# A two-layer graph attention kernel: own rows added by VectorE in the early sums, and written by ScalarE into opened accumulators in layer 0

## Chip, cores and metric

The kernel runs on one core of one Trainium2 chip. The metric is device time in microseconds of that core. A core has five engines with a queue each, worked off in order: TensorE (PE; PEld is its weight load), VectorE (DVE), ScalarE (ACT), GpSimd (POOL) and SyncE (SP). SP issues plain transfers, POOL the gathers of rows by index. Sixteen DMA engines move the data. TensorE sums into PSUM banks of 512 f32 columns.

## What is computed

N = 3327 nodes with D = 1024 features, a symmetric 0/1 adjacency with ones on its diagonal and about 17 ones in a row. Layer 0 is attention with 8 heads of 128 columns, layer 1 with one head. After each comes a residual add and a layer norm. Cut to what matters:

```python
# layer 0
h = (x @ W).reshape(C, H, D); h_heads = jnp.transpose(h, (1, 0, 2))
e = alpha_src[:, :, None] + alpha_dst[:, None, :]
e = jnp.where(e >= 0, e, NEG_SLOPE * e)            # 0.2
e = jnp.where(adj[None] == 0, -jnp.inf, e)
out = jnp.einsum('hij,hjd->hid', softmax(e, axis=-1), h_heads)
x = _layernorm(x + out)
# layer 1: the same with one head, leaky 0.2, and relu(attention @ h)
x = _layernorm(x + layer1(x))
```

The attention of a node is a weighted sum over its neighbours and over itself. The "own row" below is the node's own row of h, weighted by the node's own, unnormalised attention weight (zero where the diagonal is zero).

## The kernel before

The rows lie in 26 tiles of 128 (NT = 26; NTH = 13). The work has three stages.

**Projection** (L512 to L927). For each tile t, `project` multiplies the turned x by W0 in three column cuts of eight matmuls; `keep` has ScalarE move the result out of PSUM, and SP stores it in the table h0_d, each row followed by exponentials of its scores. `load_mask` brings a tile's adjacency as bytes with POOL's queue into one of three buffers, 416 KB. Three generators run beside the projection, and `pace()` (L629), called after every second matmul, gives them their turn. I call each call of `pace()` a slot: there are twelve per tile. In a slot:

- `counting` (L580) clears a mask's diagonal and sums it on ScalarE (L348), then packs it on VectorE (L355). It gets a turn in every third slot.
- `listing` (L592) finds a tile's neighbours: VectorE searches maxima (L307, L309), ScalarE and TensorE spread them, and the lists go to idx, tgt and re_d. It takes seven steps a tile, 187 in all, and `pace` sets how many are due: 3/7 of them in the first half of the projection, the rest in the second.
- `sums_so_far` (L646), from tile 13 on, forms for the EARLY = 17 first tiles the part of layer 0 that comes from neighbours in the first half of the rows. A tile has two blocks of four gathers from h0_d (L660, buffers near and far); per block `weights` computes e on VectorE (L677, L678, L681) and `sums` adds up 32 small matmuls for each half of the heads (L690). Then ScalarE copies both banks of the sum to z and the denominators to dens (L738, L739), and SP stores z in half_d (L740). A tile takes nine slots.

**Layer 0** (`pipeline`, L1322 on, with the class Layer0, L1059). The tiles come in an order that mixes early tiles (blocks 2, 3 and the end block 4; the other two are in half_d) and nine late ones (all five blocks). A block is four gathers of 128 rows of 4160 bytes (the end block one), into one of five buffers; `send` issues a gather as soon as a buffer is free. For a tile, `prepare` is called in the middle of the tile before: it loads x (y), the tile's own rows of h0_d (own, L1075) and, for an early tile, half_d (half, L1078). At the tile's first block `own` computes the own weights on VectorE (L1084 to L1090), and `scale_own` has ScalarE scale the own rows by head (L1097). `sums` has TensorE multiply the weights of a block with its rows (L1147; the end block at L1138), and in the second and third block adds the scaled own rows and the half sum to the accumulators by an f32 matmul with the identity (L1130). The denominators lie in den. `finish` divides, adds the residual, normalises, computes layer 1's scores, and SP stores the row in y_d (L1190).

**Layer 1** (class Target, L1199 on) gathers rows of y_d in five blocks per tile (L1258), then multiplies the normalised sum by W1 (L1290).

The scheduler's order is that of the program: everything runs in a manual schedule, so each engine's queue is the order in which these generators issue. A wait in one engine's queue holds everything behind it on that engine.

The lines around L1130 in `sums` of layer 0:

```python
if j in (1, 2):
    for rows_ in (self.h, self.half) if self.t < EARLY else (self.h,):
        nc.tensor.matmul(
            self.acc[j - 1].rearrange("p h d -> p (h d)"), ident, rows_[:, (j - 1) * HALF : j * HALF],
            start=False, stop=False,
        )
elif j == 3:
    nc.tensor.matmul(self.acc[0][:, 0, :1], ident_b, none_b, start=False, stop=False)
```

Of the kernel before, what the change touches and what calls it, by code (L numbers as in the profile page):

```python
# [19 lines left out]
P = 128  # L20
# [6 lines left out]
def kernel(  # L27
# [102 lines left out]
    dens = const.tile([P, EARLY, H], F32, name="dens")  # L130
    io_t = const.tile([P, P], F32, name="io_t")

    near = [const.tile([P, NG, HG], F32, name=f"near{b}") for b in range(HB)]

# [377 lines left out]
    with ExitStack() as own, tc.manual_schedule():  # L512
# [14 lines left out]
        def load_mask(t):  # L527
            if t < NT:
                ads[t] = masks[t % 3]
                if t == NT - 1:  # L530
                    nc.vector.memset(ads[t].bitcast(I32), 0)
                    nc.vector.memset(ads[t][:, :1], 1.0)
                for r in pieces(t):
                    nc.gpsimd.dma_start(ads[t][r, :N], adj[at(t, r), :])
# [94 lines left out]
        def pace():  # L629
# [3 lines left out]
            if n % 3 == 0:  # L633
                next(counts, None)
            first = 3 * total // 7
# [10 lines left out]
        def sums_so_far():  # L646
# [52 lines left out]

            res = [listed(0), listed(1)]  # L700
            for _ in range(3):
                yield
            for n in range(2):
                fetch(n)
                yield
                yield
                yield
# [4 lines left out]
            for s in range(EARLY):  # L712
                acc = part.bank("L", [P, 2, 4, DH], "part")
                made = []
                for b in range(HB):
                    n = s * HB + b
                    val = src[n % 3]
                    made.append(weights(val, b, res[0], oh))
                    yield
                    if n:  # L720
                        fetch(n + 2)
# [4 lines left out]
                    if b == 0:  # L726
                        yield
                        yield
# [7 lines left out]
                z = part.sbuf("z", [P, 2, 4, DH], 1)  # L736
                for n in range(2):
                    nc.scalar.activation(z[:, n], acc[:, n], AF.Copy)  # L738
                nc.scalar.activation(dens[:, s, :], den, AF.Copy)  # L739
                nc.sync.dma_start(half_d[s], z.rearrange("p n h d -> p (n h d)"))  # L740
# [5 lines left out]
                yield  # L746

# [19 lines left out]
        masks = [pool.tile([P, NP], U8, bufs=1, name=f"ad{n}") for n in range(3)]  # L767
# [107 lines left out]
        for t in range(3, NT):  # L875
# [3 lines left out]
            if t == 12:  # L879
# [11 lines left out]
            if t == 16:  # L891
                nc.gpsimd.tensor_copy(loop, own_a)
# [79 lines left out]
    def sparse(own):  # L972
# [7 lines left out]
        grows = pool.tile([P, NT, H], F32, bufs=1, name="grows")  # L980
        nc.scalar.activation(grows, sd0[:, :, 0, :], AF.Exp, scale=1 - SLOPE)
# [9 lines left out]
        none_b = pool.tile([P, 1], BF16, name="none_b")  # L991
        nc.vector.memset(none_b, 0.0)
# [66 lines left out]
        class Layer0:  # L1059
# [9 lines left out]
            def prepare(self):  # L1069
# [4 lines left out]
                self.h = sbuf("own", [P, HW0], 2)  # L1074
                nc.sync.dma_start(self.h, h0_d[self.t * P : (self.t + 1) * P, :HW0])  # L1075
                if self.t < EARLY:
                    self.half = sbuf("xT", [P, KT, P], 2, "half").rearrange("p k q -> p (k q)")
                    nc.sync.dma_start(self.half, half_d[self.t])  # L1078

            def own(self):  # L1080

                t, h = self.t, self.h
                es, total = sbuf("es0", [P, 2, H], 2).rearrange("p a h -> a p h")
                nc.vector.tensor_tensor(es, grows[:, t, :], h[:, D : D + H], OP.mult)  # L1084
                nc.vector.tensor_tensor(es, es, h[:, D + H :], OP.max)
                nc.vector.tensor_scalar(es, es, loop[:, t : t + 1], None, op0=OP.mult)
                self.es = self.total = es
                if t < EARLY:
                    self.total = total
                    nc.vector.tensor_tensor(total, es, dens[:, t, :], OP.add)  # L1090

            def scale_own(self):

                h = self.h
                for n in range(H):
                    d = slice(n * DH, (n + 1) * DH)
                    nc.scalar.activation(h[:, d], h[:, d], AF.Copy, scale=self.es[:, n : n + 1])  # L1097

            def begin(self):
                self.acc = [bank("A", [P, 4, DH], "acc") for _ in range(2)]  # L1100
# [22 lines left out]
            def sums(self, b):  # L1123
# [4 lines left out]
                if j in (1, 2):  # L1128
                    for rows_ in (self.h, self.half) if self.t < EARLY else (self.h,):
                        nc.tensor.matmul(  # L1130
                            self.acc[j - 1].rearrange("p h d -> p (h d)"), ident, rows_[:, (j - 1) * HALF : j * HALF],
                            start=False, stop=False,
                        )
                elif j == 3:
# [10 lines left out]
                for h in range(H):  # L1145
                    for g in range(NG):
                        nc.tensor.matmul(  # L1147
                            self.acc[h // 4][g * GT : (g + 1) * GT, h % 4, :], e[:, g, h, :], rowsof[:, g, h, :],
                            start=first and h % 4 == 0, stop=False,
# [16 lines left out]
            def finish(self):  # L1166

                ri = sbuf("ri", [P, H], 2)
                nc.vector.tensor_tensor(ri, self.den, self.total, OP.add)
# [29 lines left out]
        class Target:  # L1199
# [29 lines left out]

            def scale_own(self):  # L1230
                pass
# [90 lines left out]
        def pipeline(items, fetches):  # L1322
# [28 lines left out]
            get(0)  # L1351
            items[0].prepare()
# [5 lines left out]
            items[0].weights(items[0].blocks[0])  # L1358
            for i, it in enumerate(items):
# [4 lines left out]
                for j, b in enumerate(it.blocks):  # L1364
# [8 lines left out]
                    if j == 0:  # L1373
                        get(i + 1)
                    if j == nb // 2 and after:
# [7 lines left out]
                    if j == 0:  # L1383
                        it.scale_own()
# [176 lines left out]
```

## Time and profile before

| | |
|---|---|
| time, median of 3 runs | 1854.35 us (1852.41 to 1872.16) |
| the profiled execution's own time | 1778.88 us |
| its span, first to last instruction | 1777.1 us |
| busy in the span: PE, DVE, ACT, POOL | 1518.3, 1150.6, 537.5, 1111.7 us |
| transferred | 592.41 MB |
| mean granted TensorE clock | 0.926 |

The profile is that of one execution. Busy time is the time that an engine executes; a wait is idle time ahead of an instruction, put down to what ended last. In lists of groups a row gives line, engine, operation, output and input, shape and count, then busy us and mean ns of one, then the idle us ahead of it and what ended it. A matmul in f32 shows as two records. In lists of waits a row gives who waited for whom, us in total, how often, and the longest. In the chain of waits a row gives its start, its us and what it was. A mean over the span hides that the three stages have different limits, so each is looked at by itself.

### The profile page before, as it was taken

To read this page: it belongs to the slowest core of one execution; us is meant where nothing else is said; L and a number is where in the kernel's file an instruction comes from. 1 tells how busy PE (TensorE), PEld (TensorE's weight loads), DVE (VectorE), ACT (ScalarE), POOL (GpSimd) and SP (SyncE) were. 2 spreads that over 40 slices of the span, in tenths; PEclk is the share of its full clock that TensorE was granted. 3 is DMA by queue.
4 is the path that set the end of the run, shared out by engine and by line. 5 is a ranking of instruction groups with operands and counts; after the bars stand their busy time and mean duration, and the time that the engine had idled before them with its cause. 6 is when DMAs were issued, how large, how long until landed. Compare 5 with 4: busy or idle time off the path is not lost.

```text
span 1777.1 us, 36731 instructions
## 1 busy us (share of the span) xinstructions
PE 1518.3 (85%) x13778; PEld 882.2 (50%) x13778; DVE 1150.6 (65%) x3125; ACT 537.5 (30%) x1602; POOL 1111.7 (63%) x1476
## 2 busy tenths in 40 slices
PE   8799999999995667666676674599999999999998
PEld 5466666666664455444554453244444444444443
DVE  6799999888873877767777775243444444444443
ACT  5678773333322233233333332011110111101110
POOL 4443358877755666656656666677676666676750
PEclk9999999999998788888788886899999999999999
DMA  7578978998888999999999999999999999999980
GB/s 195 100 138 167 163 170 302 319 314 319 296 303 331 407 411 408 394 384 406 395 397 393 385 402 365 355 395 403 396 393 386 394 390 396 401 401 395 386 345 36
DMA packets 189050, 592.41 MB, mean 333 GB/s; under 512 B 37069, under 2 KB 47079, under 8 KB 188864
## 3 DMA queue, kind: packets, MB, share of 16 engines
q0 software_dynamic: 131056, 458.88, 72.6%
q1 hardware_dynamic: 57650, 130.84, 19.8%
q8 instruction: 111, 1.82, 0.4%
q14 instruction: 75, 0.61, 0.1%
q10 hardware_dynamic: 158, 0.26, 0.0%
HBM read 590.02 MB, written 53.33 MB: 362 GB/s over the span
## 4 chain that ended last, share of the span: by engine, by line
PE 42%; DMA 18%; DVE 4%; issue 1%; ACT 1%; POOL 1%; DVEq 0%; SPq 0%; POOLq 0%; ACTq 0%
PE mm L1290 21%; PE acc L1258 13%; DMA src<-h_d,idx 7%; DMA own<-h_d 4%; PE acc L1147 3%; DMA near<-h_d,idx 3%; PE acc L1130 3%; DVE e L1115 2%; PE tr L195 1%; DMA src<-y_d,idx 1%; DMA near<-y_d,idx 1%; ACT own L1097 1%; DMA end<-h_d,idx 1%; DVE pr L1002 1%; PE acc L1138 1%
## 5 line engine op out<-in xcount | busy, mean ns | idle before, releaser
L545 PE MATMUL mm<-wt,xT 128*128 128x347 f32 (+1 forms) x1248 | 408.0, 468 | 2.1 <-DMA wt<-in_L_gnn_W_dram 1.5
L1290 PE MATMUL mm<-wt,xT 128*128 128x512 f32 x832 | 387.6, 604 | 0.0
L1036 POOL DMA_INDIRECT src<-y_d,idx x240 | 244.6, 1019 | 95.0 <-issue 32.7
L545 PEld LDWEIGHTS mm<-wt,xT 128*128 128x128 f32 x1248 | 225.7, 192 | 116.7 <-issue 18.4
L1036 POOL DMA_INDIRECT src<-h_d,idx x168 | 180.9, 1077 | 112.4 <-PE acc L1147 25.2
L1290 PEld LDWEIGHTS mm<-wt,xT 128*128 128x128 f32 x832 | 149.7, 189 | 199.1 <-issue 194.1
L1293 DVE SCALAR_TENSOR_TENSOR o<-mm,y 128x512 f32<-128x512 f32 x52 | 36.0, 692 | 317.1 <-PE mm L1290 317.1
L1036 POOL DMA_INDIRECT near<-y_d,idx x176 | 178.9, 1017 | 90.6 <-PE acc L1258 29.7
L1130 PE MATMUL acc<-own,ident 128*128 128x512 f32 x104 | 80.4, 865 | 118.8 <-ACT own L1097 115.2
L1036 POOL DMA_INDIRECT near<-h_d,idx x104 | 116.1, 1117 | 65.1 <-DMA src<-h_d,idx 13.9
L198 ACT ACTIVATE xT<-tr 128x512 f32<-128x512 f32 x104 | 63.2, 609 | 254.1 <-PE tr L195 254.0
L1272 ACT ACTIVATE z<-y,ri 128x342 f32<-128x342 f32 (+1 forms) x78 | 39.5, 569 | 300.5 <-DVE ri L1268 300.5
L660 POOL DMA_INDIRECT near<-h_d,idx x96 | 105.2, 1096 | 36.2 <-issue 24.4
L1120 ACT ACTIVATE w<-way 128x32 f32<-128x32 f32 (+1 forms) x96 | 18.5, 192 | 350.4 <-DVE e L1115 168.6
L1115 DVE TENSOR_TENSOR e<-oh,way 128x1024 f32<-128x1024 f32 x96 | 117.2, 1221 | 8.4 <-DVE way L1113 0.5
L1147 PE MATMUL acc<-src,e 128*32 128x128 f32 x2688 | 103.4, 318 | 17.6 <-DVE e L1115 17.6
L1258 PE MATMUL acc<-src,es 128*32 128x342 f32 (+1 forms) x1440 | 116.2, 454 | 0.2
L1258 PE MATMUL acc<-near,es 128*32 128x342 f32 (+1 forms) x1056 | 90.1, 476 | 28.0 <-DVE es L1249 28.0
L1147 PEld LDWEIGHTS acc<-src,e 128*32 128x32 f32 x2688 | 88.1, 129 | 47.1 <-DVE e L1115 31.9
L1147 PE MATMUL acc<-near,e 128*32 128x128 f32 x1792 | 65.8, 309 | 23.0 <-DVE e L1115 12.2
L348 ACT ACTIVATE junk<-ad 128x1664 uint8<-128x1664 uint8 x52 | 82.9, 1594 | 5.6 <-POOL ad L337 4.0
L1130 PEld LDWEIGHTS acc<-own,ident 128*128 128x128 f32 x104 | 20.4, 245 | 124.6 <-ACT own L1097 123.9
(238 smaller groups left out, 2577.8 us busy)
## 6 DMA issues: line engine op xcount, KB each, us to landing
own<-h_d SPq DMA_DIRECT2D x26, 520.0 KB
y_d<-y SPq DMA_DIRECT2D x26, 514.0 KB
y<-y_d SPq DMA_DIRECT2D x26, 514.0 KB
h_d<-ht SPq DMA_DIRECT2D x25, 520.0 KB
x<-in_x_dram SPq DMA_DIRECT2D x25, 512.0 KB
y<-in_x_dram SPq DMA_DIRECT2D x25, 512.0 KB
out_dram<-o SPq DMA_DIRECT2D x25, 512.0 KB
ad<-in_adj_dram POOLq DMA_DIRECT2D x25, 415.9 KB
```

The lines of the kernel that those rows point to most:

```text
L198: nc.scalar.activation(part, tr, AF.Copy)
L348: nc.scalar.activation(junk, ad[:, n * THR : (n + 1) * THR], AF.Copy, accum_out=self.d[:, n : n + 1])
L545: nc.tensor.matmul(acc, xT[t][:, k, :], wt[:, k, CUTS0[c] : CUTS0[c + 1]], start=k == 0, stop=k == KT - 1)
L660: nc.gpsimd.indirect_dma_start(out=src[n % 3][:, g, :], out_offset=None, in_=h0_d[:THR, :], in_offset=bass.IndirectOffsetOnAxis(ap=idx[:, ...
L1036: nc.gpsimd.indirect_dma_start(out=s[:, g, :w], out_offset=None, in_=table[:n, :], in_offset=bass.IndirectOffsetOnAxis(ap=idx[:, t, b * NG ...
L1115: nc.vector.tensor_tensor(e, oh.unsqueeze(2).to_broadcast([P, ng, H, wide]), wp.unsqueeze(3).to_broadcast([P, ng, H, wide]), OP.mult,)
L1130: nc.tensor.matmul(self.acc[j - 1].rearrange("p h d -> p (h d)"), ident, rows_[:, (j - 1) * HALF : j * HALF], start=False, stop=False,)
L1147: nc.tensor.matmul(self.acc[h // 4][g * GT : (g + 1) * GT, h % 4, :], e[:, g, h, :], rowsof[:, g, h, :], start=first and h % 4 == 0, stop= ...
L1258: nc.tensor.matmul(self.acc[c][to, :m], es[:, g, :], s[:, g, CUTS[c] : CUTS[c + 1]], start=b == 0, stop=b == EB,)
L1272: nc.scalar.activation(z[:, cut], self.res[:, cut], AF.Copy, scale=ri[:, 1:2])
L1290: nc.tensor.matmul(acc, xT[:, k, :], wt1[:, k, half], start=k == 0, stop=k == KT - 1)
L1293: nc.vector.scalar_tensor_tensor(o[:, half], acc, 0.0, res[:, half], op0=OP.max, op1=OP.add)
```

## The change

For the early sums, SP loads each tile's own rows of h0_d into one of two buffers (`own_row`), ScalarE scales them by head with weights computed once for all tiles (`own_terms`, own_e), and VectorE adds the sums in PSUM to them (`settle`), in place of ScalarE's copy. The first half of the head columns is settled behind the tile's last sums, the second one slot later, ahead of the next tile's weights. half_d then holds the early sum with the own row in it, and own_e the denominators.

In layer 0 a tile loads one row block instead of up to two: half_d for an early tile, h0_d for a late one (`load_own`, at the first block of the tile before). In the last block of the tile before, TensorE writes zeros over both accumulators with a bf16 matmul (`open`), and ScalarE writes into them the half sum as it is or the own rows scaled by head (`lay`). The tile's first matmul adds to that. The matmuls with the identity and the own weights computed per tile are gone; the one-column zero matmul comes in the blocks 1 to 3 of a tile's list except the end block.

The pacing is changed with it: counting gets two of five slots in place of one of three, listing has 2/5 of its steps in the first half in place of 3/7, all masks but the last are counted before the early sums begin, the diagonal is loaded at tile 5 (12 before) and converted at tile 11 (16 before), and the three mask buffers are one tile, of which the first part later serves as the second own-row buffer.

```diff
@@ masks, pacing
-                ads[t] = masks[t % 3]
+                ads[t] = masks[(t + 1) % 3]
...
-            if n % 3 == 0:
+            if n * 2 % 5 < 2:
                 next(counts, None)
-            first = 3 * total // 7
+            first = 2 * total // 5
@@ own weights, once for tiles lo to hi
+    def own_terms(lo, hi, mids):
+
+        e, score = own_e[:, lo:hi, :], sd0[:, lo:hi, 1, :]
+        for mid, scale in zip(mids, (1.0, SLOPE)):
+            nc.scalar.activation(mid, score, AF.Exp, scale=scale)
+        nc.scalar.activation(e, sd0[:, lo:hi, 0, :], AF.Exp, scale=1 - SLOPE)
+        nc.vector.tensor_tensor(e, e, mids[0], OP.mult)
+        nc.vector.tensor_tensor(e, e, mids[1], OP.max)
+        nc.vector.tensor_tensor(e, e, loop[:, lo:hi].unsqueeze(2).to_broadcast([P, hi - lo, H]), OP.mult)
@@ early sums
+            def own_row(s):
+                nc.sync.dma_start(own_rows[s % 2], h0_d[s * P : (s + 1) * P, :D])
+
+            def scale(s, n):
+                for h in range(4 * n, 4 * n + 4):
+                    d = slice(h * DH, (h + 1) * DH)
+                    nc.scalar.activation(
+                        own_rows[s % 2][:, d], own_rows[s % 2][:, d], AF.Copy, scale=own_e[:, s, h : h + 1]
+                    )
+
+            def settle(s, n):
+                half = own_rows[s % 2][:, n * HALF : (n + 1) * HALF]
+                nc.vector.tensor_tensor(half, acc[:, n].rearrange("p h d -> p (h d)"), half, OP.add)
+                if n == 1:
+                    nc.vector.tensor_tensor(own_e[:, s, :], own_e[:, s, :], den, OP.add)
+                    nc.sync.dma_start(half_d[s], own_rows[s % 2])
+
+            need(NT - 2)
...
             for s in range(EARLY):
...
+                    if b == 0 and s:
+                        settle(s - 1, 1)
                     made.append(weights(val, b, res[0], oh))
                     yield
+                    if b == 0:
+                        scale(s, 0)
                     if n:
                         fetch(n + 2)
...
                     if b == 0:
+                        scale(s, 1)
                         yield
+                        if s + 1 < EARLY:
+                            own_row(s + 1)
...
-                z = part.sbuf("z", [P, 2, 4, DH], 1)
-                for n in range(2):
-                    nc.scalar.activation(z[:, n], acc[:, n], AF.Copy)
-                nc.scalar.activation(dens[:, s, :], den, AF.Copy)
-                nc.sync.dma_start(half_d[s], z.rearrange("p n h d -> p (n h d)"))
+                if s == EARLY - 1:
+                    yield
+                settle(s, 0)
@@ layer 0
+            def load_own(self):
+                self.h = sbuf("own", [P, D], 2)
+                h0 = h0_d[self.t * P : (self.t + 1) * P, :D]
+                nc.sync.dma_start(self.h, half_d[self.t] if self.t < EARLY else h0)
...
+            def open(self):
+
+                self.acc = [bank("A", [P, 4, DH], "acc") for _ in range(2)]
+                for acc in self.acc:
+                    nc.tensor.matmul(
+                        acc, zero_b, ident_b.unsqueeze(1).to_broadcast([P, 4, P]), start=True, stop=False
+                    )
+
+            def lay(self):
+
+                for n, acc in enumerate(self.acc):
+                    rows_ = self.h[:, n * HALF : (n + 1) * HALF].rearrange("p (h d) -> p h d", h=4)
+                    if self.t < EARLY:
+                        nc.scalar.activation(acc, rows_, AF.Copy)
+                        continue
+                    for h in range(4):
+                        at_h = own_e[:, self.t, 4 * n + h : 4 * n + h + 1]
+                        nc.scalar.activation(acc[:, h, :], rows_[:, h, :], AF.Copy, scale=at_h)
...
-                if j in (1, 2):
-                    for rows_ in (self.h, self.half) if self.t < EARLY else (self.h,):
-                        nc.tensor.matmul(
-                            self.acc[j - 1].rearrange("p h d -> p (h d)"), ident, rows_[:, (j - 1) * HALF : j * HALF],
-                            start=False, stop=False,
-                        )
-                elif j == 3:
+                if 0 < j < 4 and b < EB:
                     nc.tensor.matmul(self.acc[0][:, 0, :1], ident_b, none_b, start=False, stop=False)
...
-                            start=first and h % 4 == 0, stop=False,
+                            start=False, stop=False,
@@ pipeline of layer 0
                     if j == 0:
                         get(i + 1)
+                        if isinstance(after, Layer0):
+                            after.load_own()
...
                     elif after and type(after) is type(it):
                         after.weights(after.blocks[0])
-                    if j == 0:
-                        it.scale_own()
+                        if isinstance(after, Layer0):
+                            after.open()
+                            after.lay()
                     it.sums(b)
```

## The prediction

> **What bounds the kernel now.** I read the slices of the span first, then busy times by stage, then the waits and transfers of the two stages that the change touches, then the groups that it removes or that resemble what it adds.
>
> ```profile
> PE   8799999999995667666676674599999999999998
> DMA  7578978998888999999999999999999999999980
> ```
>
> PE is full for 12 slices of 44 us, half full for 14, and full again to the end; the DMA digits stay at 9 from slice 14 on. So the middle is not PE's. The same by stage (first column the stretch in us, then its length, then busy us and instructions of PE, PEld, DVE, ACT, POOL, granted clock, DMA share, GB/s):
>
> ```profile
> 0.00:270.00 270.00, 247.22 (x1042) 160.24 (x1042) 229.67 (x644) 193.21 (x573) 121.88 (x378) 0.98 0.79 158
> 270.00:545.00 275.00, 259.28 (x3067) 175.71 (x3068) 228.25 (x612) 95.33 (x366) 202.99 (x347) 0.99 0.89 309
> 545.00:575.00 30.00, 12.16 (x252) 10.51 (x254) 9.48 (x29) 4.56 (x17) 15.96 (x15) 0.76 0.87 326
> 575.00:1095.00 520.00, 353.30 (x5713) 257.00 (x5712) 388.27 (x963) 162.25 (x478) 331.43 (x306) 0.80 1.01 395
> 1095.00:1140.00 45.00, 20.09 (x175) 8.27 (x175) 17.62 (x55) 7.18 (x16) 28.06 (x27) 0.73 0.93 355
> 1140.00:1777.10 637.10, 626.25 (x3540) 270.51 (x3538) 277.31 (x824) 75.00 (x153) 411.34 (x406) 0.99 0.94 366
> ```
>
> The projection (0 to 545) is PE's, 92 to 94% busy, with DVE close behind at 83 to 85%. Layer 0 (575 to 1095) is bound by transfers: share 1.01, PE at 68%. Layer 1 (from 1140) is PE's at 98%, and the change has nothing there. In layer 0 the waits and the transfers say:
>
> ```profile
> PE acc L1130 <- ACT own L1097: 115.2, 24, 13.9
> DVE es L1084 <- DMA own<-h_d: 46.1, 17, 13.2
> DVE way L1112 <- DMA src<-h_d,idx: 34.5, 12, 4.4
> ```
>
> ```profile
> GB/s 397 413 410 414 410 413 410 409 411 405 392 387 394 412 414 381 341 414 410 403 408 387 382 414 401 376 387 387 396 414 393 377 382 402 406 402 390 333 344 409
> DMA packets 63016, 211.68 MB, mean 396 GB/s; under 512 B 9227, under 2 KB 12580, under 8 KB 62950
> ```
>
> PE waits 115 us for the scaled own row, and DVE 46 us for the load behind it, but the queues stay full meanwhile: slices at 409 to 414 GB/s are the common case, and the mean loses 4% to dips. The chain of waits shows one such turn, a load that lands late and the matmuls that wait for it:
>
> ```profile
> 633.78 9.32 DMA own<-h_d
> ...
> 647.02 2.08 PE acc L1130 x2
> ```
>
> So a PE wait removed here is worth only what it adds to the transfer rate, and a byte removed is worth its time.
>
> **Two rules of the skill.** The Trainium skill, "PSUM — Partial Sum Buffer", section "The four PSUM rules", says that a ScalarE write leaves PSUM's written bits alone, so a seed is added to only where an earlier matmul has set them. That is what the two zero matmuls per tile in open() pay for; no row of this trace shows a seeded bank. The forecast takes the opening at full price. The Trainium skill, "DMA: Bandwidth & Descriptors", section "Where 436 GB/s comes from", gives about 358 GB/s as HBM's limit for a core and 435 for the ports. This trace has 395 mean and slices at 414, which decides: I price bytes at 395 to 405.
>
> **The change, part by part: layer 0.** Removed on PE, ACT and DVE, and the rows that price what comes:
>
> ```profile
> L1130 PE MATMUL acc<-own,ident 128*128 128x512 f32 x104 | 80.4, 865 | 118.8 <-ACT own L1097 115.2 <-DMA src<-h_d,idx 3.6
> L1130 PE MATMUL acc<-half,ident 128*128 128x512 f32 x68 | 47.6, 792 | 0.0
> L1097 ACT ACTIVATE own<-own,es 128x128 f32<-128x128 f32 x208 | 63.2, 389 | 0.0
> L738 ACT ACTIVATE z<-part 128x512 f32<-128x512 f32 x34 | 18.5, 600 | 44.2 <-PE dd L732 25.1 <-PE part L690 12.9 <-issue 6.2
> L1293 DVE SCALAR_TENSOR_TENSOR o<-mm,y 128x512 f32<-128x512 f32 x52 | 36.0, 692 | 317.1 <-PE mm L1290 317.1
> ```
>
> Bytes: 26 own loads of 532,480 B and 17 half loads of 524,288 B are 22.76 MB; afterwards there are 26 loads of 524,288 B, 13.63 MB. That is 9.13 MB less of the 205.4 MB that 520 us at 395 GB/s carry. At the same rate it saves 9.13 MB / 395 GB/s = 23 us. If the own chain's going lifts the mean to 405, the stage is 196.3 / 405 = 485 us, 35 us less. I take 29. PE loses 128 us of L1130 and gains 52 zero matmuls. Their nearest row is the 128x168 bf16 at 221 ns, the f32 512 columns are 0.96 us per bank (four records in 1.91 us), so 12 to 50 us, say 16: PE has 167 us idle in the stage, which hides either. One-column zero matmuls (180 ns) go from 26 to 3 for each of 9 late and 1 for each of 17 early tiles, 44: 3 us more, hidden the same way. The new wait: the first sums of a tile need ACT's lay, queued behind the copy of that tile's first weights (L1120), which needs its gather. ACT takes 2 x 0.6 us for an early tile and 2.43 us for the eight scalings of a late one (the L1097 run of eight takes that), so PE can start 1.2 to 2.4 us after the weights instead of at once, at most 17 x 1.2 + 9 x 2.4 = 42 us; the current tile's end-block sums (16 records, about 2 us) cover most, and PE's idle time the rest. If transfers did not cover it, it would still stand against the 115 us removed. On SP the own load goes to the tile's start, one half tile earlier, ahead of the y load and behind the y_d store that is already waited for; it gets a whole tile (20 us) against a landing of 8.5 to 11 us in the chain. At the stage's start the first lay needs its load (7 us) and 2.4 us: first sums near 580 instead of 575, but the second block waited until 583 for the same load before. I charge 1 us, own_terms included.
>
> **The projection.** DVE gains two adds of 512 columns out of PSUM per early tile, by L1293 0.69 us each (below by nothing, since the same width out of SBUF takes 0.68 to 0.73 in L1052 and L498), and one of 8 columns, 0.19: 1.57 us. ACT gives up 1.2 us of L738 and 0.17 of the denominators and gains eight scalings, 2.43: 1.1 us more per tile, in a stretch where it is 35% busy. The first=2/5 pacing puts off listing: by the order of instructions 14 tiles are listed behind the first early weights, 13 before. A tile's listing is about 14 us of DVE summed by its rows, 13 with overlaps. So DVE in 270 to 545: 228 + 15 x 1.57 + 13 = 265 of 275 us. That leaves 10 us for its waits, which were:
>
> ```profile
> DVE kq L495 <- ACT xs L482: 16.6, 5, 5.3
> DVE w L677 <- DMA near<-h_d,idx: 13.7, 8, 3.0
> PE part L690 <- DVE e L681: 7.4, 6, 2.1
> ```
>
> 4.8 of the 13.7 lie behind 545. If both kinds stay, 25.5 - 10 = 16 us longer; if only the gathers' 9 stay, nothing. I take 8. DVE also waits for PE at each settle, and what follows on its queue (marks, a listing step, the second settle, the next weights) is what PE wants three slots later; that is in the 16. DVE's relief comes ahead: 240 to 270 was DVE's (4.7 us busy of every 5; PE waited 2.4 us for mvg behind DVE and 2.3 us for e), worth up to 4.7. Counting at 2/5 instead of 1/3 of the slots adds a fifth to the 72 us of mask sums (L348, L350) that ACT has in 100 to 250, 14 us on 119 of 150: 89%, costing 0 to 6 us of PE waiting for its evictions. The masks' loads and the 4-byte diagonal at t=5 share the queues at 0.87, with three masks in flight: in the same 0 to 6. I take the first part at -2. The 17 own-row loads, 8.9 MB, lift 309 to 341 GB/s over 275 us; below the 387 to 408 that its better slices reach, so hidden but for the gathers' waits. The tail (545 to 575) swaps two ACT copies for two adds: 0. Stage: +6, from -4 to +22.
>
> **Sum.** -29 + 1 + 6 = -22. The profiled execution took 1778.88 us around its span of 1777.1; it becomes 1757. The runs' median, 1854.35, lies 75 us above it, a gap that I leave as it is: 1832.
>
> **The rivals.** *DVE takes back the gain*: the projection grows by 16 to 22 us and layer 0 gives only the bytes, -23: 1854 - 23 + 1 + 19 = 1851. For it: DVE at 96%; against it: 100 to 240 ran with DVE at 92% and PE at 99%. *Layer 0 gives more*: rate 410, 479 us, -41, and the projection even: 1814. *Slower, by ACT waiting for the own row*: scale(s) stands on ACT ahead of the projection's evictions and transposes, so if the row is late PE stops for its banks. The load is issued six slots ahead, 2 us each (half stores come 18 us apart, nine slots), so 12 us; landings were 8.5 to 11 us in layer 0's fuller queues. Each us above 12 costs 17 us. At 14.4 us it turns to more than 1% slower (22 + 18.5 = 40.5 / 17 = 2.4); at 15 us, 51 us: 1883. *It frees nothing*: layer 0 is limited by how soon buffers come free rather than by bytes, saves 8, and the projection pays 6: 1853.
>
> **How the numbers follow.** Mine 0.47, DVE 0.18, more 0.10, ACT waiting 0.13, nothing 0.12. A measurement tells about 1%, 18.5 us, from no change. Mine is faster by over 1% in about 0.44 of its 0.47, being spread from 1820 to 1840; with layer 0's larger gain that is 0.54; within 1% 0.31 from the rest, slower 0.15. The range: 1812 for the bigger gain, 1862 beyond the two cases of no gain.
>
> **What would show it.** DMA bytes of layer 0 near 202 MB in place of 211.68 and the stage near 492 us; no wait of PE for a scaled own row; DVE over 93% busy from 270 to 545 with that stage's end up to 20 us later. Wrong if ACT waits for the own-row load in the projection, if PE's waits for L681's successor pass 25 us, or if layer 0 shortens by less than 15 us.

## The result, and the profile after

The changed kernel takes 1878.76 us (median of 19 runs, 1869.52 to 1883.74) beside 1855.49 of the kernel before on the same chip (19 runs): ratio 1.0116, interval 1.0099 to 1.0132 (95%; intervals stand in square brackets below). It is 1.2% slower, where 1832 was forecast.

These times need one thing to be understood: the chips that ran this study are of two kinds. In the first series of runs, and in one later, the kernel before takes 1855 to 1858 us; in four other series, on three chips, it takes 1780 to 1781. (One chip was used in two series and was of the same kind in both; what makes the kinds differ isn't known.) By its span of 1777.1 and its layer 1 of 630 us the profile of before shown above is from a chip of the second kind, while the profile of after is from one of the first. They can't be subtracted. Where a number is compared below, both sides are from one kind, called the 1855 chips and the 1780 chips. On the 1780 chips the change makes no difference: 1782.46 beside 1781.3, ratio 1.0004 [0.9992, 1.0016].

The page of after (1855 chip), its slices of 46.8 us, and the transfers:

```profile
PE   8799998888897577777777777499999999999998
DMA  7589967778887999999999999799999999999990
GB/s 185 96 140 164 196 220 264 266 264 288 298 294 260 348 357 373 393 361 380 400 351 373 378 382 386 285 373 382 384 380 375 382 383 378 393 387 382 368 355 34
DMA packets 189048, 592.18 MB, mean 316 GB/s; under 512 B 37069, under 2 KB 47079, under 8 KB 188864
```

The bytes of the whole program hardly change (592.41 to 592.18 MB): what layer 0 no longer loads, the early sums load. Layer 0 (640 to 1170) runs at 377 GB/s here, in a second profile on a 1855 chip at 373, not at 395, and PE's digit is 7. The waits of PE in the whole span (who for whom, us, times, longest):

```profile
PE acc L1194 <- issue: 102.1, 271, 1.1
PE part L700 <- DVE e L691: 34.4, 15, 6.9
```

"issue" is time in which PE waited for nothing that the trace shows; the first row's matmuls of layer 0 have 102 us of it, in 271 gaps of at most 1.1 us. On a 1780 chip the list of the same program has, for the same matmuls:

```profile
PE acc L1194 <- issue: 1.0, 2, 0.7
```

Like with like, on a 1780 chip, the changed kernel by stage (columns as in the prediction's table):

```profile
0.00:270.00 270.00, 245.55 (x1013) 159.88 (x1014) 215.41 (x603) 188.88 (x553) 113.46 (x357) 0.96 0.78 156
270.00:575.00 305.00, 270.77 (x3108) 181.95 (x3107) 262.13 (x704) 121.31 (x475) 218.01 (x368) 0.98 0.89 312
575.00:600.00 25.00, 10.19 (x238) 8.97 (x235) 9.30 (x22) 3.96 (x17) 11.45 (x10) 0.70 0.92 335
600.00:1095.00 495.00, 283.32 (x5554) 243.35 (x5554) 369.78 (x873) 145.98 (x377) 327.33 (x305) 0.79 1.01 395
1140.00:1780.50 640.50, 631.98 (x3601) 273.19 (x3596) 280.45 (x835) 77.15 (x157) 414.13 (x410) 1.00 0.94 367
```

Layer 0 fills 495 us in place of 520 at the same rate, 395 GB/s. The projection's second part fills 305 in place of 275 to 280. To compare all runs alike I use one mark, the start of the projection's last matmul (with wt and xT), and the time from there to the first multiplication by W1 in layer 1. The last column runs from that multiplication to the end.

| us | span | last projection matmul | to layer 1 | layer 1 |
|---|---|---|---|---|
| before, three profiles (1780) | 1777.7 to 1782.1 | 549.4 to 551.5 | 597.1 to 600.5 | 630 |
| after, two profiles (1780) | 1779.8, 1780.5 | 575.3, 574.6 | 573.6, 576.2 | 630 |
| after, two profiles (1855) | 1871.1, 1876.7 | 607.8, 608.2 | 610.7, 616.3 | 652 |

On the 1780 chips the means go from 550.6 to 575.0 at the mark (24.4 later) and from 599.2 to 574.9 behind it (24.3 less): what layer 0 gives, the projection takes. (The profile shown ahead of the prediction has 546.9 and 600.5; with it the two differences are 25.3 and 24.6.) Behind the mark 223.61 MB move in place of 232.81, 9.2 MB less where 9.13 were forecast; at 395 GB/s that is 23 us.

### The profile page after: what moved, and what is told of

The parts are those of the page before. It is cut to its first block, busy times and chain, and to the rows that moved or that the text cites. A ratio compares the mean times of both kernels' runs of the same rounds, so it can differ in the third digit from the quotient of the medians.

```text
span 1871.1 us, 36430 instructions
## 1 busy us (share of the span) xinstructions
PE 1603.7 (86%) x13693; PEld 919.6 (49%) x13693; DVE 1155.9 (62%) x3090; ACT 542.8 (29%) x1593; POOL 1093.2 (58%) x1476
## 2 busy tenths in 40 slices
DMA packets 189048, 592.18 MB, mean 316 GB/s; under 512 B 37069, under 2 KB 47079, under 8 KB 188864
## 4 chain that ended last, share of the span: by engine, by line
PE 54%; issue 8%; DVE 3%; DMA 1%; POOL 0%; ACT 0%; another core or an unknown queue 0%; SPq 0%; DVEq 0%; ACTq 0%; POOLq 0%
PE mm L1334 20%; PE acc L1302 14%; PE acc L1194 13%; PE acc L1185 3%; PE tr L205 1%; PE acc L1137 1%; DVE pr L1052 1%; PE den L1205 1%; DMA own<-h_d 0%; DMA near<-y_d,idx 0%; DMA av<-in_L_gnn_a_dram 0%; PE tr L1241 0%; DVE y L1222 0%; DVE e L1168 0%; POOL near L1086 0%
## 5 line engine op out<-in xcount | busy, mean ns | idle before, releaser
L555 PE MATMUL mm<-wt,xT 128*128 128x347 f32 (+1 forms) x1248 | 415.1, 475 | 2.8 <-DMA wt<-in_L_gnn_W_dram 2.8
L1194 PE MATMUL acc<-src,e 128*32 128x128 f32 x2688 | 170.0, 307 | 71.3 <-issue 62.0
L1086 POOL DMA_INDIRECT src<-h_d,idx x168 | 175.7, 1046 | 94.0 <-issue 30.5
L1194 PEld LDWEIGHTS acc<-src,e 128*32 128x32 f32 x2688 | 100.3, 120 | 130.8 <-issue 118.8
L1194 PE MATMUL acc<-near,e 128*32 128x128 f32 x1792 | 115.9, 310 | 46.6 <-issue 40.0
L1302 PE MATMUL acc<-src,es 128*32 128x342 f32 (+1 forms) x1440 | 126.9, 455 | 3.7 <-issue 2.9
L1302 PE MATMUL acc<-near,es 128*32 128x342 f32 (+1 forms) x1056 | 97.1, 469 | 26.0 <-DVE es L1293 23.0
L1194 PEld LDWEIGHTS acc<-near,e 128*32 128x32 f32 x1792 | 67.7, 122 | 87.5 <-issue 79.5
L700 PE MATMUL part<-near,e 128*32 128x128 f32 x1408 | 60.8, 309 | 35.6 <-DVE e L691 26.6
L1302 PEld LDWEIGHTS acc<-src,es 128*32 128x32 f32 x1440 | 47.3, 109 | 73.4 <-issue 51.4
```

Source lines behind the costliest of these rows:

```text
L555: nc.tensor.matmul(acc, xT[t][:, k, :], wt[:, k, CUTS0[c] : CUTS0[c + 1]], start=k == 0, stop=k == KT - 1)
L700: nc.tensor.matmul(acc[g * GT : (g + 1) * GT, h // 4, h % 4, :], e[:, g, h, :], vals[:, g, h, :], start=b == 0 and h % 4 == 0, stop=b == H ...
L1086: nc.gpsimd.indirect_dma_start(out=s[:, g, :w], out_offset=None, in_=table[:n, :], in_offset=bass.IndirectOffsetOnAxis(ap=idx[:, t, b * NG ...
L1194: nc.tensor.matmul(self.acc[h // 4][g * GT : (g + 1) * GT, h % 4, :], e[:, g, h, :], rowsof[:, g, h, :], start=False, stop=False,)
L1302: nc.tensor.matmul(self.acc[c][to, :m], es[:, g, :], s[:, g, CUTS[c] : CUTS[c + 1]], start=b == 0, stop=b == EB,)
```

## The experiments

**Is it the pacing?** The kernel before with the new pacing alone (e2_pace), and one more profile each of before (e0) and after (e1) for the stages.

```diff
-            if n % 3 == 0:
+            if n * 2 % 5 < 2:
-            first = 3 * total // 7
+            first = 2 * total // 5
```

> The kernel before, profiled again beside the others on one chip. Its profiled execution took 1778.88 us where its 19 timed runs lie between 1849.73 and 1872.16, while the changed kernel's profile agrees with its runs (1872.8 of a median of 1878.76). If that profile was an exception, this one has a span near 1850 and its own waits of TensorE for issue in layer 0 (then 17 us for L1147, against 198 us for the same line after the change) rise with it. If the change causes the issue waits, the span of this profile is near 1780 and the waits stay below 30 us.

> The changed kernel, profiled again on the same chip, so that the stages are compared like with like: span near 1872, first gather of layer 0 near 630. Theory A (the projection pays): layer 0 begins 25 us or more later than in the kernel before on this chip and lasts as long or shorter. Theory B (the opening pays): layer 0 itself is 20 us longer.

> The kernel before with the new pacing alone: counting in two of five slots, 2/5 of the listing in the first half, the masks counted before the early sums, the diagonal loaded at tile 5. Theory A1 (the pacing lengthens the projection): ratio 1.010 or more, layer 0 begins 20 us later. Theory A2 (VectorE's adds and ScalarE's scalings lengthen it) and theory B: 0.997 to 1.004.

On a 1780 chip: before 1783.8 and after 1781.48 (one execution each), pacing 1781.1, ratio 1.0000 [0.9987, 1.0013]. As after itself has a ratio of 1.00 on these chips, it is the mark that decides: the last projection matmul of e2_pace starts at 549.9, of after at 575.3. The pacing alone costs nothing. Of the theories in e1_after, A has the stages right: the projection ends 24 us later, and layer 0 is shorter.

**Is it the opening?** After, with layer 0's zero matmuls and ScalarE's writes replaced by one f32 matmul with the identity per bank.

```diff
-                        nc.scalar.activation(acc[:, h, :], rows_[:, h, :], AF.Copy, scale=at_h)
+                if j in (1, 2):
+                    nc.tensor.matmul(
+                        self.acc[j - 1].rearrange("p h d -> p (h d)"), ident, self.h[:, (j - 1) * HALF : j * HALF],
+                        start=False, stop=False,
+                    )
```

> The changed kernel, with layer 0's opening undone: no zero matmuls and no ScalarE writes into the accumulators; the one row block (half_d, or the scaled own rows) is added with the identity matmul in the second and third block as before. The projection and the bytes are those of the change. Theory B (the opening and the wait for ScalarE's writes cost): 0.985 to 0.995 of the kernel before, as the bytes saved then show. Theory A (the projection costs): 1.008 to 1.015, no better than the change.

1781.55, ratio 1.0003 [0.9995, 1.0011], between what the two theories expected; but the mark is at 575.0 and layer 1 comes 573.7 us behind it, both as in after. Yet the opening has waits of its own, in layer 0 of after (1780 chip):

```profile
PE acc L1194 <- ACT acc L1146: 54.7, 16, 5.1
PE acc L1194 <- ACT acc L1150: 44.8, 10, 6.7
```

Some 100 us of PE waiting for ScalarE's writes took the place of 115 for the scaled own row; without the opening, in e3_ident, these waits are gone (PE waits 125 us for VectorE's e instead) and the stage is as long. With the queues full (share 1.01 in the table above) and the rate unchanged, the 24 us of layer 0 are those of its bytes.

**Which part of the projection?** On a 1855 chip: the first half settled one slot later too, with the second at the next tile's start (e4_late); ScalarE copying the sums out instead of VectorE adding, with the early tiles' own rows left out (e5_acts); the early sums opened and seeded as in layer 0 (e6_seed); and after again.

```diff
# e4_late
-                settle(s, 0)
...
+                        settle(s - 1, 0)
                         settle(s - 1, 1)
# e5_acts
-                nc.vector.tensor_tensor(half, acc[:, n].rearrange("p h d -> p (h d)"), half, OP.add)
+                nc.scalar.activation(half, acc[:, n].rearrange("p h d -> p (h d)"), AF.Copy)
...
-                        settle(s - 1, 1)
...
                 settle(s, 0)
+                settle(s, 1)
# e6_seed
+                    nc.scalar.activation(
+                        acc[:, h // 4, h % 4, :], own_rows[s % 2][:, d], AF.Copy, scale=own_e[:, s, h : h + 1]
+                    )
```

> The changed kernel with the first half settled together with the second, one slot later, so that VectorE no longer waits for TensorE ahead of the marks and a listing step. Loop theory (the projection's 24 us come from VectorE waiting for TensorE's sums and TensorE then for VectorE's e): half or more of the 24 us comes back, 0.990 to 0.994 of the kernel before. Work theory (VectorE simply has too much to do): at most 4 us, 0.998 to 1.001.

> The changed kernel with ScalarE copying both banks out, as before the change, in place of VectorE's adds; it leaves out the own rows of the early tiles. Loads of own rows, scalings and pacing stay. VectorE theory (its adds, by work or by waiting, are the 24 us): 0.984 to 0.989, layer 0 begins within 4 us of the kernel before. Rival (the own-row loads or ScalarE's scalings are the cost): 0.995 or more, layer 0 still begins 15 us or more later.

> The same result by another way: in the early sums too, TensorE opens the banks with zeros and ScalarE writes the scaled own rows into them; ScalarE copies the sum out as before the change, and VectorE adds only the denominators. ScalarE has 3.6 us per tile of 18, TensorE 0.4 us more. If VectorE's adds are the cost, this keeps layer 0's gain: 0.984 to 0.990. If a new wait of TensorE for ScalarE's writes takes their place: 0.995 or more.

> The changed kernel, timed on this chip beside the three. If the chip is like the one where the kernel before takes 1780 us: 0.998 to 1.003 (one look gave 1781.48 against 1780.36). If it is like the one where it takes 1855 us: 1.010 to 1.013, and the profile shows waits of TensorE for issue in layer 0 near 100 us, as that profile did.

Measured, before at 1858.0: late 1863.88, 1.0044 [1.0021, 1.0068]; acts 1878.16, 1.0114 [1.0073, 1.0155]; seed 1924.51, 1.0370 [1.0326, 1.0414]; after 1878.12, 1.0109 [1.0072, 1.0145]. All but the last were expected with a 1780 chip in mind, so their ratios are to be read beside after's 1.0109. Moving the first addition by a slot, with all its work kept, is 14 us faster than after and brought the last projection matmul from 608.2 to 595.0; VectorE's idle time ahead of the two additions fell from 55 to 22 us. That is over half of what the change loses here, as the theory of the loop expected. The seed has a new wait from 270 to 630:

```profile
PE part L700 <- ACT part L725: 58.5, 15, 7.5
```

PE waits 58 us for ScalarE's writes, as the rival in its expectation said. And acts, by its number, went as the rival said too (the loads or ScalarE's scalings are the cost), but it is no clean test: its edit put the small addition of denominators on VectorE at the tile's end, where the first addition had stood, and VectorE was idle 67 us ahead of it. The wait stayed while 23 us of work went, and nothing was gained. Loads and scalings are tested further below.

**One turn of the loop.** Changed kernel, 1780 chip, the timeline of PE and then of VectorE from 384 to 397 us (start, us, what; in brackets the wait). The first row is the tile's last sums for the first half of the heads, the second for the second half:

```profile
384.28 1.08 PE L700 MATMUL part<-near,e 128*32 128x128 f32 x32 [1.92 <-DVE e L691]
...
386.89 1.08 PE L700 MATMUL part<-near,e 128*32 128x128 f32 x32
387.79 0.29 PE L782 MATMUL dd<-w,oh 128*32 128x8 f32 x16
388.01 3.77 PE L555 MATMUL mm<-wt,xT 128*128 128x347 f32 x12
394.37 1.26 PE L700 MATMUL part<-far,e 128*32 128x128 f32 x32 [2.59 <-DVE e L691]
```

```profile
385.12 0.43 DVE L317 MAX8 pack<-cols 128x8 f32<-128x256 f32 x1
388.17 0.69 DVE L727 TENSOR_TENSOR ad<-part,ad 128x512 f32<-128x512 f32 x1 [2.62 <-ACT re L495]
388.78 0.41 DVE L678 TENSOR_TENSOR oh<-io_t,tgt 128x256 f32<-128x256 f32 x1
...
391.98 0.68 DVE L727 TENSOR_TENSOR ad<-part,ad 128x512 f32<-128x512 f32 x1
392.58 0.15 DVE L729 TENSOR_TENSOR own_e<-own_e,dd 128x8 f32<-128x8 f32 x1
...
393.09 1.23 DVE L691 TENSOR_TENSOR e<-oh,w 128x1024 f32<-128x1024 f32 x1
```

VectorE stands 2.62 us before the first addition. PE ended the tile's last sums at 387.97 (386.89 + 1.08), and the addition starts at 388.17. (The row puts the wait down to another write that ended about then. But in all ten waits ahead of additions in this profile, 21.5 us together, the addition starts 0.12 to 0.21 us behind the tile's last sums.) The first addition reads only the first half of the heads, whose last sums ended at 385.36, so it waited 2.6 us for sums that it doesn't read. In the kernel both banks are one tile, `acc`; whether two tiles would shorten the wait was not run. Everything behind moves: marks, a listing step, the second addition, and at 393.09 the products e, whose absence then costs PE 2.59 us. In the list of waits from 270 to 575, before and then after (h1_before and h3_after, one 1780 chip), PE waits for these products 20 times instead of 8, and 19 us more; VectorE's old waits (kq, gathers) nearly go, and those ahead of the additions (L727) come:

```profile
DVE kq L495 <- ACT xs L482: 16.6, 6, 5.3
PE part L690 <- DVE e L681: 14.7, 8, 4.1
...
DVE w L677 <- DMA near<-h_d,idx: 13.3, 7, 3.8
```

```profile
PE part L700 <- DVE e L691: 33.6, 20, 2.6
...
DVE row L727 <- ACT re L495: 6.6, 2, 4.0
DVE row L727 <- PE dd L782: 4.2, 3, 2.6
DVE kq L505 <- ACT xs L492: 4.2, 2, 3.8
...
DVE ad L727 <- PE dd L782: 4.0, 3, 2.4
...
DVE ad L727 <- ACT re L495: 2.6, 1, 2.6
...
DVE w L687 <- DMA far<-h_d,idx: 1.1, 2, 0.8
```

**Wait or work?** ScalarE copies the sums out again, and the own row is added to the copy two slots later, behind the next tile's products, by VectorE (f2_zadd) or GpSimd (f3_zpool). With one buffer for own rows their load moves behind that, and their scaling into the tile's second block.

```diff
+            def evict():
+                for n in range(2):
+                    half = own_rows[0][:, n * HALF : (n + 1) * HALF]
+                    nc.scalar.activation(half, acc[:, n].rearrange("p h d -> p (h d)"), AF.Copy)
...
+                nc.vector.tensor_tensor(half, half, row, OP.add)
```

> The kernel before once more, for its profile on this call's chip. If the chip is of the kind on which it takes about 1858 us, its layer 1 should stand at 652 us and its projection and layer 0 together at 1204, which the earlier call gave only as a difference; if TensorE's shortage of instructions belongs to the chip and not to the change, its share of waits for nothing shown (issue) in layer 0 is as large as after's, about 100 us. On a chip of the other kind: 575 and 576 us for projection and layer 0.

> After, but ScalarE copies the sums out as before the change, and VectorE adds the own row to the copy two slots later, from SBUF. VectorE's work stays (two 128x512 additions a tile), its waits on TensorE go, and TensorE's wait for VectorE's additions before the next tile's sums goes too. The theory of the loop (VectorE waits for the tile's last matmul, the next tile's products queue behind it, TensorE waits for those): projection 576 to 582 instead of 599 on a chip of the 1780 kind, ratio 0.988 to 0.992; on one of the 1858 kind ratio 0.995 to 1.001, under the 1.0044 of e4_late. The theory of the work (VectorE simply has some 25 us more to do in a stage that it fills): projection stays at 595 to 600, ratio 1.000 (1.010 on the other kind).

> As f2_zadd, but GpSimd makes the two additions. By the loop theory the same as f2_zadd within 4 us, since VectorE was no longer late. By the work theory, 12 to 20 us less than f2_zadd, VectorE's additions (18 x 2 x 0.68 us) being gone. A rival: the additions (2.35 us for 128x1024 where GpSimd makes one) stand ahead of gathers in GpSimd's queue, and a late gather delays TensorE: 5 to 15 us more than f2_zadd.

This series ran on a 1780 chip: before 1781.35; zadd 1781.38, 0.9998 [0.9982, 1.0014]; zpool 1795.73, 1.0073 [1.0054, 1.0091]. (The projection's 576 to 599 us in the expectation run to the start of layer 0; the mark used here is at 575 in after and at 570.4 in zadd.) The ratio of zadd is the one that the theory of the work named, but its waits, 270 to 575, show that it settles nothing:

```profile
ACT ad L721 <- DMA ad<-h_d: 41.4, 11, 12.4
...
PE part L700 <- DVE e L691: 16.9, 9, 3.2
```

PE's wait for VectorE is halved, but ScalarE now stands 41 us before own rows that land late: the prediction's rival, made by my own edit. zpool came out where its rival had it, 14 us above zadd. The addition on GpSimd, and then VectorE's products from 270 to 586 (count, then shortest, median and longest ns):

```profile
L727 POOL TENSOR_TENSOR row<-row,ad x34: 1255/1276/2337, 291.8 to 607.4; 128x512 f32<-128x512 f32 x34
```

```profile
L691 DVE TENSOR_TENSOR e<-oh,w x32: 1224/1226/4020, 271.5 to 582.0; 128x1024 f32<-128x1024 f32 x32
```

GpSimd needs 1.28 us (median) where VectorE needs 0.68, and a VectorE product took up to 4.02 us, in zadd at most 1.27. Four of the 32 took over 2 us, each while GpSimd was adding (the longest from 557.55 to 561.57, beside additions from 557.99 to 560.47). The Trainium skill, "SBUF — State Buffer", section "Who interferes with whom", says that a tensor_tensor with both inputs in SBUF contends with what GpSimd reads there; the products are such, and these rows agree. But the four together lost under 6 us; where the rest of the 14 comes from, late gathers as the rival had it or something else, isn't shown.

**The three causes apart.** g1_z2 is zadd with two buffers for own rows, asked for a tile ahead and scaled in the first block again. From it g2_noadd leaves out the additions (and so the early tiles' own rows), g3_noscale the scaling by the own weight, and g4_dma has a DMA add.

```diff
# g1_z2
-                nc.sync.dma_start(own_rows[1], h0_d[s * P : (s + 1) * P, :D])
+                nc.sync.dma_start(own_rows[1 + s % 2], h0_d[s * P : (s + 1) * P, :D])
# g2_noadd
-                nc.vector.tensor_tensor(half, half, row, OP.add)
# g3_noscale
-                    nc.scalar.activation(
-                        own_rows[1 + s % 2][:, d], own_rows[1 + s % 2][:, d], AF.Copy, scale=own_e[:, s, h : h + 1]
-                    )
# g4_dma
+                    nc.gpsimd.dma_start(own_rows[1 + s % 2], own_rows[0], accum_op=OP.add)
```

> As f2_zadd, but with two buffers for own rows, so that a row is again asked for a tile ahead, as in after. If f2_zadd was held by late rows (ACT waits 41 us for them), the projection's last multiplication ends at 556 to 562 us on a chip of the 1780 kind instead of 570, ratio 0.991 to 0.995. If VectorE's work or ScalarE's is what costs, it stays within 3 us of f2_zadd: ratio 0.998 to 1.001.

> g1_z2 without VectorE's two additions a tile (the early tiles' own rows are left out of the output). If VectorE's work is the cause: 18 to 23 us less than g1_z2 (34 x 0.68 us is 23), projection's last multiplication at 549 to 553, ratio 0.985 to 0.989. If ScalarE's scalings are: no more than 5 us less than g1_z2.

> g1_z2 without ScalarE's eight scalings a tile (the own rows of early tiles are added unscaled). 136 scalings of 0.40 us are 54 us of ScalarE, which has 120 of 305 us busy. If ScalarE's work is the cause, because what VectorE and TensorE wait for (xs, cnt, place_of) stands behind the scalings in its queue: 12 to 22 us less than g1_z2. If VectorE's work is: within 4 us of g1_z2.

> g1_z2, but a DMA issued by GpSimd adds the copied sums to the own row, in place of VectorE. If VectorE's work is the cause and 0.5 MB a tile more of DMA is covered (the queues were 87% busy in this stage): as g2_noadd plus up to 5 us, ratio 0.986 to 0.992, faster than both kernels. If the transfers of gathers suffer from it (18 x 0.5 MB at 396 GB/s are 23 us of the queues): as g1_z2 or slower, 1.000 to 1.010.

| 1780 chip, before 1780.75 | median us | ratio | last projection matmul | to layer 1 |
|---|---|---|---|---|
| g1_z2 | 1773.89 | 0.9955 [0.9938, 0.9972] | 562.0 | 579.1 |
| g2_noadd | 1764.70 | 0.9903 [0.9876, 0.9931] | 553.8 | 576.5 |
| g3_noscale | 1774.01 | 0.9955 [0.9939, 0.9971] | 565.0 | 577.3 |
| g4_dma | 1794.10 | 1.0069 [1.0054, 1.0084] | 570.3 | 590.7 |

ScalarE's scalings cost nothing, as the theory of VectorE's work has it. The additions cost 8 to 9 us (by the mark and by the median), between what the two theories named and far from the 23 of their durations. g2_noadd still loads and scales the own rows and copies the sums, and its mark is 3 us behind that of before, so loads, scalings and copies together cost at most those 3. The late own rows of zadd cost 6 to 8 (570.4 there; 562.0 here and 564.0 in a later run on zadd's chip). In z2 VectorE's turn, same place as above, has no wait at the additions, which stand behind the products (in the whole profile 4.3 us of waits ahead of them, in place of 21.5):

```profile
388.41 1.23 DVE L691 TENSOR_TENSOR e<-oh,w 128x1024 f32<-128x1024 f32 x1
389.56 1.29 DVE L727 TENSOR_TENSOR row<-row,ad 128x512 f32<-128x512 f32 x2
```

The adding DMA misses its hope. Its waits from 270 to 586:

```profile
ACT ad L721 <- DMA ad<-h_d: 40.6, 12, 5.8
...
DVE w L687 <- DMA near<-h_d,idx: 13.3, 6, 3.6
```

Own rows and gathers land later again, as the second half of its expectation said. Layer 1 comes another 12 us later behind the mark than in z2; the runs don't show why.

**Side by side once more**, meant for a 1855 chip:

> The kernel before, for its stages on this call's chip. On a chip of the 1858 kind: layer 1 652 us, projection and layer 0 together 1204; if the loss in the projection is of the same size there, projection 606 to 612 and layer 0 592 to 598, so that the change gains only 4 to 8 us in layer 0 there. On the 1780 kind: 575 and 576, as seen.

> g1_z2 again. On the 1780 kind ratio 0.994 to 0.998 as measured. On the 1858 kind, if the wait of VectorE is the same part of the loss there: about 20 us under after, ratio 0.997 to 1.002; if layer 0 gains little there, 0.999 to 1.004.

> The changed kernel timed beside h2_z2. On the 1780 kind 0.999 to 1.002 (one look gave 1781.5 beside 1780.4); on the 1858 kind 1.009 to 1.013 as measured twice.

It was a 1780 chip: before 1781.3; z2 1774.88, 0.9961 [0.9945, 0.9977]; after 1782.46, 1.0004 [0.9992, 1.0016]. On the 1780 chips z2 beats before by 0.4%, twice, and after here by as much; on a 1855 chip it wasn't run. Its gain at the mark is larger (11 to 13 us), but some 4 us of it are lost again behind the mark (579 us to layer 1 in place of 575), which wasn't traced.

## Why the prediction was wrong

*Layer 0* was right in kind and near in size. Forecast: bytes alone 23, taken 29, since the rate might rise. Measured 24 on the 1780 chips; the rate stayed at 395 GB/s. The term that was mis-sized is the 6 us of a better rate. The opening's wait, put at up to 42 us, came to about 100, and was hidden as said (e3_ident).

*The projection* is the step that failed: "I take 8", "Stage: +6, from -4 to +22". On the 1780 chips it was +24. VectorE's work was right: 265 forecast, 262 measured, an addition 0.68 us for 0.69. That the old waits would give way to work was right too: of some 30 us for kq and gathers about 5 were left (in z2, without the new wait, 17 to 18). Wrong was "DVE also waits for PE at each settle ... that is in the 16". The settle's wait is no part of the old waits that the 16 were worked out from: it is new, 17.8 us from 270 to 575 and 21.6 in all, it should have been a term of its own, and it closed a loop PE, VectorE, PE. So VectorE was 88% busy from 270 to 545, not the 93% and more of a full engine, while PE's wait for L681's successor, L691, passed the 25 us that the prediction had named as a sign of being wrong (33.6).

Taking the wait off the path, with the additions put behind the products, gave back 11 to 13 us of the 24 (575.0 to 562.0 and 564.0), leaving out the additions 8 more, and some 3 remain. So with the wait gone the projection is about 12 us longer than before, within the range that the prediction had for work and old waits. The 11 to 13 are the wait and the place behind the products together; e4_late, which leaves the additions ahead of the products and only lets PE finish first, gave back 13 on a 1855 chip, which suggests that it is mostly the wait.

*The first part*, taken as -2, can't be told from nothing: with the pacing alone the last projection matmul starts at 549.9, between the three profiles of before. The rest of that term, more listing in the second half, is in the same zero.

*The rivals.* "DVE takes back the gain" was what happened on the 1780 chips, with +24 and -24 for its +16 to +22 and -23; its sum was 1851 beside 1854. "ACT waiting for the own row" did not happen in the change, but did in zadd, where rows were asked for later, and in g4_dma, where they landed later.

*The 75 us between the profiled execution and the median*, left as it was, was no offset: the two belong to different kinds of chip. On the 1855 kind after is 20 to 23 us slower than before (1.0109 and 1.0116), not even with it. There PE's instructions start further apart: beside the 102 us of gaps in layer 0, the 960 matmuls of 342 columns in layer 1 last 451 ns each on both kinds, but together cover 88.8 us in place of 80.1, as fewer overlap. The granted clock doesn't tell the kinds apart (0.919 and 0.927 against 0.917 and 0.919 for after). VectorE's idle time ahead of its additions is 53 to 55 us there, not 21.5, and e4_late, which cuts it to 22, takes back 14 of the 20 us. So the same wait carries most of the loss there too, as far as that one run shows.

What layer 0 gains on that kind stays open, as no profile of the kernel before exists on such a chip. In layer 0 of after the chain of waits runs there through the matmuls of L1194 (46.5%) and gaps without a cause (24.2%), on a 1780 chip through gathers (28.3% and 11.3%). If PE is the limit there, fewer bytes would be worth less; but the change also takes the 128 us of L1130 off PE, which would be worth more.

## What to carry to other kernels

Before an addition out of PSUM replaces a copy by another engine, ask what stands behind it on its queue: if the engine that fills the bank also needs the next thing on that queue, a copy by a third engine keeps the two apart. Idle time of an in-order engine takes up new work only in part: here, on an engine 83% busy, 23 us of additions cost 8 to 9. A wait that the new work brings with it is a term of its own: here it cost more than the work, 11 to 13 us. Ask which sums the waiting instruction really reads. Compare stages only between profiles of one chip kind, and look at the profiled execution's own time before subtracting.

## What the runs showed that was not expected

- Two kinds of chip: 1780 and 1855 us for one program, layer 1 630 and 652, with 102 us of PE gaps in layer 0 that nothing in the trace explains, against 1.0.
- An addition that reads one PSUM bank started only 0.12 to 0.21 us behind the last sums of the other bank, in all ten waits of one profile; in the turn shown its own bank had been ready 2.6 us earlier.
- GpSimd's 128x512 f32 addition took 1.28 us, VectorE's 0.68, and beside it a VectorE product of 1.23 us took up to 4.02.
- A bank opened by a bf16 zero matmul and then written by ScalarE was added to by the later matmuls; 52 openings took 19.6 us of PE (377 ns each by the sum, 464 by the mean of the row), where 16 was forecast.
